# The last group's LoRA products computed densely over all experts, from tables kept in the place of W

## The chip, the cores and the metric

The kernel runs on one NeuronCore of a Trainium2 chip. TensorE (PE) multiplies matrices into PSUM, VectorE (DVE) and ScalarE (ACT) work on SBUF and PSUM, GpSimd (POOL) does small elementwise work and issues the indirect DMAs, SyncE (SP) issues most of the other DMAs. The metric is the device time of one execution in microseconds (us), as the median of several runs. Everything is in fp32, except the attention's parts, which are marked fp32r.

## The reference, cut to what matters

A graph-attention layer and a router-gated LoRA layer, each with a residual, for 128 batch elements of 128 rows by 1024 columns. The change concerns the second layer:

```python
def _gates(cls, router_w):                       # cls: row 0 of each batch element
    logits = jnp.einsum('bh,eh->be', cls, router_w)
    top_vals, top_idx = jax.lax.top_k(logits, 2)
    mask = jnp.full_like(logits, -jnp.inf)
    mask = mask.at[rows, top_idx].set(top_vals)
    return jax.nn.softmax(mask, axis=1)          # zero outside the two best of 8 experts

x = x + gnn(layernorm(x), adj, W, a)             # attention, 128 batch elements
z = layernorm(x)
gates = _gates(z[:, 0, :], router_w)             # (128, 8)
down = jnp.einsum('blh,erh->bler', z, lora_down) # 8 experts, rank 16
x = x + z + jnp.einsum('bler,ehr,be->blh', down, lora_up, gates)
```

(The last line is the reference's two residual steps written as one.) Only two of the eight gates of a batch element are nonzero, so two experts, 32 rows of the 128 of all experts, are enough for each of them.

## The kernel before, in words

A batch element i is one tile of 128 rows by 1024 columns (`xn`). Tiles go in pairs: pair q holds tiles 2q and 2q+1, and there are 64 pairs (`NQ`). Four tiles make a group g, and there are 32 groups (`NG`). The projection of a pair by W is a Strassen scheme with seven products (`product_1` to `product_7`, L312 to L343); each is eight fp32 matmuls (L293) of 128x128 weights with 260 moving columns. W lies in SBUF in seven blocks of one tile `w_sb` (B11, B21, B22, T1, T2, T3, NT4; L82, L83). Product 1 is the only one to read B11, product 2 the only one to read B21.

The order of the work is written out by hand. The loop over q at L633 fills eight lists, `gaps[0]` to `gaps[7]`, with small steps; L684 to L688 run the list of a gap and then the next product of pair q, so that the steps stand between the products. From q of 1 on, the order of the products is 1, 6, 2, 5, 7, 3, 4. While pair q is projected, pair q-1 goes through the attention: `attention_weights` (L376), `attend` (matmuls L406), `update` (L416, the exponential L423, L424, L425), `second_stats` (mean and variance, L229, and on POOL L233 to L443), and `turn`, which brings the tile's transpose to `y_t` by a DMA transpose (L458, issued on SP) and a copy on ACT (`rejoin`, L462). The last pair has no products after it and goes another way: `turn_at_end` (L465) transposes on PE (L472) and copies on ACT (L473). `join` (L478, ACT) adds the normalised tile to the residual.

A group's LoRA steps follow its second pair. `logits` and `choose` (L481 to L515) find the two best experts; `spread` (L520) lays them out by tile; `ratio` (L526, ACT) and `weigh` (L532 to L535, DVE) make the two gates. In the next pass of the loop `fetch` (L547) spreads the experts' numbers over the partitions (`to_rows`, L540 to L544), computes row numbers (L552, L555) and has POOL issue nine indirect DMAs: eight that gather each slot's down table from a DRAM table (`down`, L558), and one that gathers the up rows (`up`, L562). `gates` brings the gates to the partitions in the same way, `ffn_down` (L577) makes the lower products with four tiles of the group side by side in the PE array (32 columns each), scales them by the gates (L583, ACT), and `ffn_up` (L593) makes the upper products, again four side by side in 32 rows each. L597 on DVE adds them to the tile, and L600 on SP stores the finished tile, 512 KB.

For groups 0 to 30 all this lies between the products of later pairs. For group 31 there are none left: passes q = 64 and q = 65 of the loop run without a product.

PSUM is in two pools: `ps_w`, two buffers for the products, and `ps_m`, four buffers for all else.

Of the kernel before, what the change touches and what calls it, by code (L numbers as in the profile page):

```python
# [8 lines left out]
F32 = mybir.dt.float32  # L9
# [5 lines left out]
ALU = mybir.AluOpType  # L15
# [10 lines left out]
def adj_ffn_kernel(  # L26
# [13 lines left out]
    nc = tc.nc  # L40
    B, N, D = x.shape
    P = 128
# [449 lines left out]
    def choose(g):  # L492

        st = GRP[g]
        both = small.tile([G, E + 1], F32, tag="lg", name="lg")
        nc.vector.tensor_copy(both, st["pl"][:G, 0:E + 1])
        lg, dev = both[:, 0:E], both[:, E:E + 1]
        top = small.tile([G, 8], F32, tag="top", name="top")
        nc.vector.max(out=top, in_=lg)

        val = small.tile([G, 2, TOP], F32, tag="val", name="val")
        first = small.tile([G, E], F32, tag="first", name="first")
        mark = small.tile([G, 2, E], F32, tag="mark", name="mark")
        for s in range(TOP):
            nc.vector.scalar_tensor_tensor(mark[:, s], lg, top[:, s:s + 1], order,
                                           op0=ALU.is_equal, op1=ALU.mult)
            if s:
                nc.vector.tensor_scalar(first, order, val[:, 0, 0:1], None, op0=ALU.is_equal)
                nc.vector.scalar_tensor_tensor(mark[:, s], first, float(-E), mark[:, s],
                                               op0=ALU.mult, op1=ALU.add)  # L510
            nc.vector.tensor_reduce(val[:, 0, s:s + 1], mark[:, s], AX.X, ALU.max)
        st["experts"] = spread(val[:, 0], "experts")
        pr = small.tile([G, 2], F32, tag="pr", name="pr")
        nc.vector.tensor_sub(pr[:, 0:1], top[:, 1:2], top[:, 0:1])
        st.update(val=val, pr=pr, dev=dev)  # L515
# [12 lines left out]
    def weigh(g):  # L528

        st = GRP[g]  # L530
        gate, pr = st["val"][:, 1], st["pr"]
        nc.vector.tensor_scalar(gate[:, 0:1], pr[:, 1:2], 1.0, None, op0=ALU.add)  # L532
        nc.vector.reciprocal(gate[:, 0:1], gate[:, 0:1])
        nc.vector.tensor_mul(gate[:, 1:2], pr[:, 1:2], gate[:, 0:1])
        st["gates"] = spread(gate, "gates")  # L535

    def to_rows(own, name):

# [62 lines left out]

    def weights_3_main():
        nc.gpsimd.tensor_tensor(w_sb[:, T3, :, :, MAIN], w_sb[:, B22, :, :, MAIN],
                                w_sb[:, T1, :, :, MAIN], ALU.subtract)
# [26 lines left out]
    for q in range(NQ + 2):  # L633
        gaps = [[] for _ in range(8)]
        if q == 0:
            prepare(gaps)
        g, part = divmod(q - 2, 2)
        ffn = 0 <= g < NG
        if ffn and not part:
            gaps[6] += [(logits, g), (choose, g)]  # L640
        if q < NQ:
            gaps[6] += [(high, q, 3), (high, q, 1)]
            gaps[7].append((high, q, 2))
        if ffn and not part:
            gaps[6].append((ratio, g))
        if 0 < q <= NQ:
            i = 2 * q - 2
            gaps[0].append((attention_weights, q - 1))
            gaps[1] += [(attend, i), (update, i)]
            gaps[2] += [(attend, i + 1), (second_stats, i)]  # L650
            gaps[3].append((second_stats, i + 1))
            if q < NQ:
                gaps[2] += [(turn, i), (update, i + 1)]
                gaps[3].insert(0, (turn, i + 1))
                gaps[4].append((rejoin, i))
                gaps[5].append((rejoin, i + 1))
            else:
                gaps[2] += [(turn_at_end, i), (update, i + 1)]
                gaps[3].insert(0, (turn_at_end, i + 1))
            gaps[5] += [(join, i), (join, i + 1)]  # L660
        if q + 1 < NQ:
            gaps[3].append((first_stats, 2 * q + 2))
            gaps[4] += [(pair_sums, q + 1), (first_stats, 2 * q + 3)]
        if ffn and part:
            gaps[0].insert(0, (fetch, g))
            gaps[0].append((weigh, g))
            gaps[3].insert(0, (gates, g))
            gaps[4].insert(0, (ffn_down, g))
            gaps[5].insert(0, (ffn_up, (g, 0)))
            gaps[6].append((ffn_up, (g, 1)))  # L670
        if q % 2 == 0 and q < NQ:
            gaps[5].append((group_adj, q // 2))
            if q // 2 + 1 < NG:
                gaps[5].append((load_adj, q // 2 + 1))
        if q < NQ:
            gaps[3].insert(0, (low, q, 0))
            gaps[6] += [(low, q, 3), (low, q, 1)]

        if q + 1 < NQ:
            load_xt(q + 1)  # L680
            load_x(q + 1)
        if q == 1:
            slot, down_row, up_row = experts()
        products = project(q) if q < NQ else iter(())  # L684
        for gap in gaps:
            for f, *args in gap:
                f(*args)
            next(products, None)  # L688
# [37 lines left out]
```

## Time and profile before

| | before |
|---|---|
| median of three runs | 1979.18 us (1979.04 to 1979.5) |
| the profiled execution | 1979.41 us, of which the trace spans 1977.4 us |
| PE busy | 1933.0 us, 98% |
| DVE, ACT, POOL busy | 1666.3, 1075.3, 857.1 us |
| mean granted PE clock | 0.99 of full speed |
| last product of the last pair begins | 1925.79 us |
| last DVE instruction ends | 1971.81 us |

The table's first rows are times of whole executions; the rest is read from one profiled execution, whose microseconds count from its first instruction. A share of busy time is a mean over the whole span: 98% for PE says that the 64 passes with products are bound by PE, and nothing of the last 50 us. In the profile an fp32 matmul shows as two PE instructions, each with its own weight load (PEld), so eight fp32 matmuls stand as x16.

### The profile page before, as it was taken

Reading aid. Unit: us, or ns where it says so; the run is one execution under the profiler, and the core shown is the slowest. Engines: PE = TensorE matmul, PEld = TensorE weight load, DVE = VectorE, ACT = ScalarE, POOL = GpSimd, SP = SyncE. Lnnn points to the kernel's source line nnn. Section 1 sums busy time; section 2 is a strip of 40 time slices with the busy share of each in tenths; the row PEclk is TensorE's granted clock in tenths of the full one; section 3 lists DMA queues with packets and bytes.
Section 4 is the critical chain, followed back from the end, with each engine's and each line's share of the span. In section 5 each row is a group of like instructions: output and inputs, shape, how many; then the busy total and the mean of one; then the engine's idle time right before and its main releaser. Section 6 shows DMA issues by size and latency. Waiting matters only on the chain.

```text
span 1977.4 us, 30159 instructions
## 1 busy us (share of the span) xinstructions
PE 1933.0 (98%) x11028; PEld 1572.8 (80%) x11028; DVE 1666.3 (84%) x3515; ACT 1075.3 (54%) x1027; POOL 857.1 (43%) x1137
## 2 busy tenths in 40 slices
PE   7999999999999999999999999999999999999994
PEld 4888888888888888888888888888888888888882
DVE  8788888888888888888888888888888888888874
ACT  0365565565565565565565565565565565555561
POOL 4353443553443553443553443554443554433532
PEclk9999999999999999999999999999999999999995
DMA  5346556556556556556656556546556656556532
GB/s 192 117 129 192 175 149 187 166 143 192 176 150 187 165 145 192 176 150 187 172 138 194 176 148 186 175 135 195 175 151 186 176 133 199 171 152 185 180 77 102
DMA packets 345221, 324.99 MB, mean 164 GB/s; under 512 B 274289, under 2 KB 279409, under 8 KB 345073
## 3 DMA queue, kind: packets, MB, share of 16 engines
q1 hardware_dynamic: 325202, 278.45, 48.2%
q0 software_dynamic: 17408, 41.96, 7.2%
q10 hardware_dynamic: 2464, 2.65, 0.4%
q8 instruction: 88, 1.44, 0.3%
q14 instruction: 59, 0.48, 0.1%
HBM read 189.31 MB, written 67.63 MB: 130 GB/s over the span
## 4 chain that ended last, share of the span: by engine, by line
PE 90%; DVE 5%; DMA 2%; ACT 1%; issue 0%; POOL 0%; POOLq 0%; ACTq 0%; DVEq 0%
PE pw L293 75%; PE ph L406 6%; PE pu L593 4%; PE pd L577 3%; DMA tt<-halves 1%; PE pb L540 1%; PE pl L486 1%; DVE xn L424 1%; DVE xn L425 1%; DVE hp L416 1%; ACT y_t L462 1%; DMA w_sb<-in_w 1%; ACT halves L456 1%; DVE w_sb L169 0%; DVE stats L229 0%
## 5 line engine op out<-in xcount | busy, mean ns | idle before, releaser
L293 PE MATMUL pw<-w_sb,xt 128*128 128x260 f32 x4096 | 947.4, 386 | 2.4 <-DVE parts L364 1.7
L293 PEld LDWEIGHTS pw<-w_sb,xt 128*128 128x128 f32 x4096 | 767.5, 190 | 148.3 <-issue 29.6
L293 PE MATMUL pw<-w_sb,s 128*128 128x260 f32 x3072 | 711.2, 385 | 4.2 <-DVE w_sb L613 3.4
L293 PEld LDWEIGHTS pw<-w_sb,s 128*128 128x128 f32 x3072 | 578.1, 190 | 117.2 <-issue 17.4
L233 POOL TENSOR_SCALAR rstd<-mv 128x2 f32<-128x2 f32 x128 | 29.0, 227 | 869.4 <-DVE mv L230 864.2
L462 ACT COPY y_t<-tt 128x2048 uint16<-128x2048 uint16 x126 | 315.1, 2505 | 77.0 <-DMA tt<-halves 76.6
L558 POOL DMA_INDIRECT down<-table,at_down x256 | 259.5, 1014 | 168.6 <-DVE e L380 89.2
L229 DVE BATCH_NORM_STATS2 stats<-xn 128x6 f32<-128x512 f32 x512 | 324.1, 675 | 5.6 <-DMA xn<-in_x 5.5
L456 ACT COPY halves<-xn 128x2048 uint16<-128x2048 uint16 x126 | 239.8, 1903 | 119.6 <-DVE xn L425 73.7
L360 ACT ACTIVATE parts<-wh,rstd 128x512 fp32r<-128x512 f32 x192 | 133.9, 716 | 227.5 <-DVE wh L301 227.5
L423 ACT ACTIVATE ex<-hp 128x1024 f32<-128x1024 f32 x128 | 135.5, 1058 | 178.2 <-DVE hp L416 171.9
L597 DVE SCALAR_TENSOR_TENSOR xn<-pu,rstd,xn 128x512 f32<-128x512 f32 x256 | 174.5, 744 | 37.4 <-PE pu L593 37.3
L416 DVE TENSOR_TENSOR hp<-ph,att 128x512 f32<-128x512 f32 x256 | 161.4, 672 | 9.9 <-PE ph L406 9.6
L425 DVE SCALAR_TENSOR_TENSOR xn<-ex,xn 128x1024 f32<-128x1024 f32 x128 | 156.8, 1225 | 14.0 <-DVE xn L424 0.9
L406 PE MATMUL ph<-parts,adj_f 128*128 128x512 f32 x512 | 164.2, 442 | 1.3 <-ACT parts L360 0.8
L424 DVE SCALAR_TENSOR_TENSOR xn<-hp,xn 128x1024 f32<-128x1024 f32 x128 | 156.9, 1226 | 4.4
L478 ACT ACTIVATE xn<-xn,off,mul 128x1024 f32<-128x1024 f32 x128 | 151.3, 1230 | 0.8 <-POOL off L443 0.8
L364 DVE SCALAR_TENSOR_TENSOR parts<-wh,rstd,parts 128x512 fp32r<-128x512 f32 x192 | 138.9, 751 | 12.5 <-ACT parts L360 12.5
L301 DVE TENSOR_TENSOR wh<-pw,u 128x520 f32<-128x520 f32 x128 | 89.1, 696 | 48.8 <-PE pw L293 45.5
L301 DVE TENSOR_TENSOR wh<-pw,p 128x520 f32<-128x520 f32 x64 | 44.8, 700 | 80.9 <-PE pw L293 80.9
L406 PEld LDWEIGHTS ph<-parts,adj_f 128*128 128x128 f32 x512 | 96.5, 189 | 20.4 <-ACT parts L360 1.2
L234 POOL TENSOR_TENSOR rstd<-rstd,half_pow 128x2 f32<-128x2 f32 x128 | 91.5, 715 | 10.6
(105 smaller groups left out, 1489.8 us busy)
## 6 DMA issues: line engine op xcount, KB each, us to landing
xn<-in_x SPq DMA_DIRECT2D x128, 512.0 KB
xt<-in_x_t SPq DMA_DIRECT2D x128, 512.0 KB
out_y<-xn SPq DMA_DIRECT2D x128, 512.0 KB
adj_f<-in_adj_t POOLq DMA_DIRECT2D x32, 256.0 KB
adj_i<-in_adj SPq DMA_DIRECT2D x32, 256.0 KB
down<-table,at_down POOLq DMA_INDIRECT x256
w_sb<-in_w ACTq DMA_DIRECT2D x8, 256.0 KB
w_sb<-in_w SPq DMA_DIRECT2D x8, 256.0 KB
```

Source lines behind the costliest of these rows:

```text
L229: nc.vector.bn_stats(st[:, h, :], X[i][:, h * HALF:(h + 1) * HALF])
L293: nc.tensor.matmul(dst[:, j, 0:QE], lhs[:, k, :], w_sb[:, rhs, k, j], start=(first and k == 0), stop=(k == KH - 1), skip_group_check=not f ...
L364: nc.vector.scalar_tensor_tensor(in_two(PARTS[q][:, 1, b]), block, rstd, in_two(PARTS[q][:, 0, b].bitcast(F32)), op0=ALU.mult, op1=ALU.sub ...
L406: nc.tensor.matmul(PH[i][h], GRP[g]["adj_f"][:, t, :], PARTS[q][:, s, NH * (i % 2) + h], start=(s == 0), stop=(s == 1))
L416: nc.vector.tensor_tensor(hp[:, h * HALF:(h + 1) * HALF].rearrange("p (h f) -> p h f", f=F), ph.rearrange("p (h f) -> p h f", f=F), att[:, ...
L424: nc.vector.scalar_tensor_tensor(xt, hp, 0.0, xt, op0=ALU.max, op1=ALU.add)
L425: nc.vector.scalar_tensor_tensor(xt, ex, 1.0, xt, op0=ALU.min, op1=ALU.add)
L456: nc.scalar.copy(halves, X[i].bitcast(U16).rearrange("p (d s) -> p s d", s=2))
L462: nc.scalar.copy(y_of(i).bitcast(U16).rearrange("p k (n s) -> p s k n", s=2), TT.pop(i).rearrange("p (s k) n -> p s k n", s=2))
L478: nc.scalar.activation(X[i], X[i], AF.Identity, bias=GRP[g]["off"][:, t:t + 1], scale=GRP[g]["mul"][:, t:t + 1])
L558: nc.gpsimd.indirect_dma_start(out=st["down"][:, j * R:(j + 1) * R].rearrange("p r k -> p (r k)"), out_offset=None, in_=table, in_offset=b ...
L597: nc.vector.scalar_tensor_tensor(y[:, cols], pu[t], st["rstd"][:, t:t + 1], y[:, cols], op0=ALU.mult, op1=ALU.add)
```

## The change

It concerns group 31, the last one, alone. Groups 0 to 30 keep their steps.

- `load_all`: in pass q = 63, after product 1, SP issues two DMAs into block B11 of `w_sb`: the down table of all experts from DRAM (512 KB, in rows of 512 B) and the up table (512 KB, in rows of 4 KB). In SP's order they stand ahead of the DMA transposes of that pass.
- `order_all`: later in that pass ACT copies the down table into block B21 in the order that a matmul wants (128x1024).
- `down_dense`: the lower products with all 128 rows of the eight experts, unscaled, into one PSUM tile `pd_all`: tiles 0 and 1 of the group together (eight matmuls with 256 columns) after the last `attend` in pass 64, tile 2 (eight with 128 columns) ahead of the last tile's transposes, tile 3 (eight with 128 columns) after `logits`.
- `gates_dense`: gates for all eight experts, zero for six, made on four partitions (L635, L638 of the new file), turned to partitions by one small matmul (L641), copied (L644) and multiplied with `pd_all` (L646, DVE, 128x512).
- `up_dense`: for each tile and each half of the columns one matmul with 128 rows and 512 columns (L656), the addition on DVE (L657), and the store of that half, 256 KB, on SP or ACT.
- Without `fetch`, `gates`, `ffn_down` and `ffn_up`, group 31 has no indirect DMA, no L540 to L555 and no L577 to L600. `weigh` moves from pass 65 to the end of pass 64.

```diff
-        st["experts"] = spread(val[:, 0], "experts")
+        if g < NG - 1:
+            st["experts"] = spread(val[:, 0], "experts")
...
-        st["gates"] = spread(gate, "gates")
+        if g < NG - 1:
+            st["gates"] = spread(gate, "gates")
...
+    block = [w_sb[:, b].rearrange("p k j c -> p (k j c)") for b in (B11, B21)]
+    up_all = block[0][:, 0:D]
+    down_of_rows = block[0][:, D:2 * D].rearrange("p (e r k) -> p e r k", e=E, r=R)
+    down_all = block[1][:, 0:D].rearrange("p (k e r) -> p k e r", e=E, r=R)
+
+    def load_all():
+        nc.sync.dma_start(down_of_rows.rearrange("p e r k -> p e (r k)"),
+                          table.rearrange("(e p) c -> p e c", p=P))
+        nc.sync.dma_start(up_all, up_t)
+
+    def order_all():
+        nc.scalar.copy(down_all, down_of_rows.rearrange("p e r k -> p k e r"))
+
+    def down_dense(g, t, n):
+        st = GRP[g]
+        if t == 0:
+            st["pd"] = ps_w.tile([P, 2, HALF], F32, tag="pw", name="pd_all")[:, 0]
+        cols = slice(t * P, (t + n) * P)
+        for k in range(KC):
+            nc.tensor.matmul(st["pd"][:, cols], down_all[:, k].rearrange("p e r -> p (e r)"),
+                             st["y_t"][:, k, cols], start=(k == 0), stop=(k == KC - 1))
+
+    def gates_dense(g):
+        st = GRP[g]
+        val = st["val"]
+        chosen = small.tile([G, TOP, E], F32, tag="chosen", name="chosen", bufs=1)
+        for s in range(TOP):
+            nc.vector.tensor_scalar(chosen[:, s], order, val[:, 0, s:s + 1], val[:, 1, s:s + 1],
+                                    op0=ALU.is_equal, op1=ALU.mult)
+        rows = work.tile([G, E, R], F32, tag="hp", name="chosen_rows")
+        nc.vector.tensor_tensor(rows, chosen[:, 0, :, None].to_broadcast([G, E, R]),
+                                chosen[:, 1, :, None].to_broadcast([G, E, R]), ALU.add)
+        pg = ps_m.tile([P, HALF], F32, tag="pm", name="pg")
+        nc.tensor.matmul(pg[:, 0:G], rows.rearrange("g e r -> g (e r)"), ident[:G, :G],
+                         start=True, stop=True)
+        gate = small.tile([P, G], F32, tag="gate_all", name="gate_all", bufs=1)
+        nc.vector.tensor_copy(gate, pg[:, 0:G])
+        st["dn"] = work.tile([P, G, P], F32, tag="s1", name="dn_all", bufs=1)
+        nc.vector.tensor_tensor(st["dn"], st["pd"].rearrange("p (t n) -> p t n", t=G),
+                                gate[:, :, None].to_broadcast([P, G, P]), ALU.mult)
+
+    def up_dense(g):
+        st = GRP[g]
+        for t in range(G):
+            y = X.pop(g * G + t)
+            for h in range(NH):
+                cols = slice(h * HALF, (h + 1) * HALF)
+                pu = ps_m.tile([P, HALF], F32, tag="pm", name="pu")
+                nc.tensor.matmul(pu, st["dn"][:, t], up_all[:, cols], start=True, stop=True)
+                nc.vector.scalar_tensor_tensor(y[:, cols], pu, st["rstd"][:, t:t + 1], y[:, cols],
+                                               op0=ALU.mult, op1=ALU.add)
+                (nc.sync, nc.scalar)[h].dma_start(out[g * G + t, :, cols], y[:, cols])
...
         if ffn and not part:
             gaps[6].append((ratio, g))
+            if g == NG - 1:
+                gaps[6] += [(down_dense, g, 3, 1), (weigh, g)]
...
-        if ffn and part:
+        if q == NQ - 1:
+            gaps[1].append((load_all,))
+            gaps[5].append((order_all,))
+        if q == NQ:
+            gaps[2].insert(1, (down_dense, NG - 1, 0, 2))
+            gaps[3].insert(0, (down_dense, NG - 1, 2, 1))
+        if ffn and part and g == NG - 1:
+            gaps[0] += [(gates_dense, g), (up_dense, g)]
+        elif ffn and part:
             gaps[0].insert(0, (fetch, g))
             gaps[0].append((weigh, g))
             gaps[3].insert(0, (gates, g))
```

## The prediction

> **What bounds the kernel now.** The change touches only the last pass with products and what follows, so I read the end of the span. First the chain of waits in order of time (start us, us, what), from 1942 us on.
>
> ```profile
> 1942.58 1.98 PE pt L472 x8
> ...
> 1948.96 0.16 DVE val L533
> ...
> 1949.51 1.10 POOL down L558
> ...
> 1958.45 2.50 DMA down<-table,at_down
> ...
> 1961.08 3.41 PE pd L577 x58
> 1964.52 0.38 ACT dn L583
> 1964.94 1.22 PE pu L593 x8
> ...
> 1969.74 2.07 DVE xn L597 x3
> ```
>
> The gates' values are ready at 1949.30. Then POOL issues nine gathers one after the other, the last needed one lands at 1960.95, and only then do the bulk of the lower products run: from 1949.5 to 1964.5 nothing else is on the path. Second, the timeline of PE and ACT in that end (start us, us, idle before in brackets).
>
> ```profile
> 1932.33 0.97 PE L406 MATMUL ph<-parts,adj_f 128*128 128x512 f32 x3 [0.49 <-DVE parts L364]
> ...
> 1937.36 1.94 PE L472 MATMUL pt<-ident,xn 128*128 128x128 f32 x8 [4.07 <-DVE xn L425]
> ...
> 1942.58 1.97 PE L472 MATMUL pt<-ident,xn 128*128 128x128 f32 x8 [3.28 <-DVE xn L425]
> ...
> 1945.96 2.37 ACT L478 ACTIVATE xn<-xn,off,mul 128x1024 f32<-128x1024 f32 x2 [0.79 <-POOL off L443]
> ...
> 1948.24 0.28 ACT L526 ACTIVATE pr<-pr,lg 4x1 f32<-4x1 f32 x1
> ```
>
> PE is idle for 4.07 us before the first tile's transposes and 3.28 us before the second's; the new products are put there. The gates' ratio (L526) stands behind ACT's two joins, not behind the logits. Third, short windows (us, busy us of PE, PEld, DVE, ACT, POOL; then clock, DMA share, GB/s).
>
> ```profile
> 1933.00:1933.50 0.50, 0.29 (x2) 0.00 (x0) 0.38 (x3) 0.00 (x0) 0.00 (x0) 0.93 0.00 0
> 1933.50:1934.00 0.50, 0.00 (x0) 0.00 (x0) 0.50 (x2) 0.00 (x0) 0.00 (x0) 0.50 0.00 0
> ...
> 1964.00:1964.50 0.50, 0.48 (x10) 0.17 (x2) 0.00 (x0) 0.00 (x0) 0.00 (x0) 0.85 0.00 0
> ...
> 1967.50:1968.00 0.50, 0.50 (x3) 0.37 (x2) 0.50 (x2) 0.00 (x0) 0.00 (x0) 0.56 0.00 0
> ```
>
> The clock falls to half at about 1933.43, rises at 1964.15 and falls at 1967.56. The last two are 3.41 us apart, and the first lies nine times 3.41 us before the second. The finished tiles leave at 401 to 410 GB/s from 1970.43 to 1975.6.
>
> **What the Trainium skill says.** "TensorE: Matmul & The Clock Gate", Part 1: the clock is full or half, decided on free-running windows of about 3.4 us; the steps above fit it. "FP8 and Floating Point Precision", TensorE Precision Notes: true fp32 takes four passes through the array. Four times 260 columns at the 2.4 GHz of the first page is 433 ns; the trace's products start every 3.5 us for eight, 437 ns each. It agrees. "TensorE: Matmul & The Clock Gate", Part 3: tiles side by side run together, so dense products give that up. The trace agrees: 32 lower products with 32 columns take 1.98 us at 1914.32. "DMA: Bandwidth & Descriptors", Bandwidth: 1 MB into SBUF takes 6.15 us when issued from GpSimd; no row of before shows such a load from SP at this place.
>
> **The change part by part**, on the trace's clock. A 260-column half matmul (one x of x16) takes 0.219 us, so 0.84 ns a column at full and 1.68 at half clock.
>
> *Loads.* Product 1 of pair 63 ends at 1901.2. SP waits for it and then issues two loads of 512 KB. Behind them on SP stand the two DMA transposes, which waited for ACT until 1908.09 in before. At the skill's 6.15 us and 1 us of issue the loads land at about 1908.5 (estimate); from below, at 406 GB/s, at 1905. One gather or transpose may be pushed by 1 us. Who would notice: pair 63's lower products at 1914.32, whose last gather was issued at 1909.46 and lands 2.5 us later (as in the tail), with 2.3 us to spare; ACT's copies of the transposes, which began at 1916.64, behind L583. I take zero, bounds 0 and +3.
>
> *order_all.* One ACT copy, 128x1024; the rows of such size are 1.06 (L423) and 1.23 us (L478). It runs between 1923.7 and 1925.6, where ACT was idle 1.25 us; behind it are two L360, whose reader on DVE (L364) starts only at 1928.52. Zero.
>
> *Lower products.* Tiles 0 and 1: 16 halves of 256 columns, 16 x 0.215 = 3.4 us at full clock from 1933.3, done at 1936.8, before 1937.36: free. With the fall at 1933.43 as in this trace: eight halves at 0.43 until the next window's end (1936.87), eight at 0.215 after it, done at 1938.6. Then the first transposes are 1.2 us late and ACT's two copies with them; ACT's exponential L423 (1940.04) stands behind these copies and ends at about 1942.2, and DVE's L425 is 0.9 us late. Tile 2: 128 columns do not hide the weight load. The nearest row is L204 of the start, the same form: 16 halves from 62.9 to 66.4, 0.233 each, so 16 x 0.233 = 3.7 us, half of it after each ACT copy (1939.07, 1939.93): done at 1942.9, 0.3 us after the second tile's transposes could start. Together the last tile's chain is 0 to 1.4 us late; the logits had 0.9 us to spare before L526 (choice done 1947.35, L526 at 1948.24). I take +0.9 for L526 in this phase, 0 in the best. Tile 3: 3.7 us from 1945.6, done at 1949.4, before the small gate matmul.
>
> *Removed.* Between L526's end (1948.52) and the first upper product (1964.94) lie 16.4 us: L540 to L555, L520, nine gathers, pd, dn. *Added in their place:* weigh, three small DVE steps (0.55 us with gaps, rows L532 to L534); two chosen and the rows (0.16, 0.2, 0.3); the matmul's round trip DVE to DVE (0.75, as L520's end to L542 at 1950.23); copy 0.16; dn_all 128x512 from PSUM 0.67 (L416's mean). With hand-overs of 0.1 the sum is 3.1 us: upper products start at 1951.65.
>
> *Upper products.* Before: 1964.94 to the last DVE end at 1971.81, 6.87 us, paced by DVE. After: 16 halves of 512 columns one after the other, 16 x 0.43 = 6.9 us, plus a drain of 0.2 and one DVE step of 0.75: 7.85 us; DVE needs 8 x 0.69 = 5.5 and is not the bound. At full clock the last DVE ends at 1959.5. In the trace's phase 0.9 later, and one window at half costs four halves' worth, 1.7 us: 1962.1.
>
> *Stores.* Before, four stores of 512 KB came at once: bytes begin 0.87 us after the first DVE end (1969.56), run 5.2 us, and the span ends 1.8 us after the last byte, 5.6 after the last DVE. Now 256 KB leave every 0.86 us, 305 GB/s, under 406: no queue, so 0.87 + 0.65 + 1.8 = 3.3 us after the last DVE. A gain of 2.3.
>
> *Sum.* End of span 1962.8 (full clock) to 1965.4 (this phase), against 1977.4: -14.6 to -12.0. The runs are about 1.8 us above the span (median 1979.18), so 1964.6 to 1967.2. I take 1966.5, as the trace's own phase is the likelier.
>
> **Rivals.** *A cold PE.* If half clock holds throughout: tiles 0 and 1 take 6.8 us (to 1940.2), the exponential ends at 1943.9, L526 at 1951.35 (2.8 late), upper products run from 1954.5 for 13.8 us, the last DVE ends at 1969.2 and the span at 1972.5: 1974.3 us. For: before ran the whole of 1933.5 to 1964 at half. Against: the new products fill PE from 1933.3 to 1949.4, and 3 us of full work raised the clock at 1964.15. *A collision of loads with the gathers of pair 63*, which holds PE at 1914.32: up to 3 us, 1969.5. Against: the gathers keep POOL's pace of 1.25 us each and the DMA share is 0.11 to 0.34 there. *Slower: the table load lands late.* ACT's second L478 of pass 63 now waits for it, and behind it stand L617, two L360 and so the last attention. It decides from 1924.7 on (1928.5 less 1.2 + 1.2 + 1.4), microsecond for microsecond. The gain of 12.7 is used up and 4 us lost at a landing of 1941.4, 40 us for 1.05 MB, 26 GB/s. For: rows of 512 B and transposes behind it. Against: the gathers have the same rows and run at 66 GB/s while held by POOL's issue; at that rate it lands at 1917.5. That group 31 keeps its fetch is excluded: the built program has nine POOL DMAs fewer.
>
> **How the numbers follow.** The forecast has 0.76 (own range 1964 to 1969), the cold PE 0.12 (1969 to 1975), the collision 0.05 (1967 to 1970), the late load 0.04 (over 1983), and 0.03 for causes that leave it within 0.2%. That bound, 4 us, is about what a measurement of this kernel can tell from no change. The range, 1963 to 1971, leaves out the late load, the worst of the cold PE and the no-change case. Faster: 0.76 + 0.05 + 0.11; same: 0.03 + 0.01; slower 0.04.
>
> **What would show it.** No POOL work after 1946; pd_all's first x16 right behind ph, ended by 1937 to 1939; the first pu at 1951 to 1953; pu as x16 in about 7 to 9 us, with DVE waiting for PE; the span's end 3.3 us after the last DVE. Wrong: a PE idle before 1926 that before doesn't have, L617 starting after 1925, or the clock at 0.5 through pu.

## The result, and the profile after

The changed kernel takes 1968.17 us (median of six runs, 1967.21 to 1969.25); the kernel before, beside it, 1979.34 us (six runs, 1979.04 to 1980.88). The ratio is 0.9941, with a 95% interval of 0.9928 to 0.9954, so the change saves 11.2 us. (A later comparison of the same two kernels, shown under "The combination, and once more", has 14.0 us.) The forecast of 1966.5 us is 1.7 us too low, and the result lies in the range of 1963 to 1971.

The profiled execution of the new kernel spans 1965.7 us (its own run took 1968.2). The chain of waits at its end (start us, us, what), against the chain of before that the prediction shows:

```profile
1948.94 1.23 ACT xn L478
1950.16 0.19 ACT pr L527
...
1951.66 0.39 PE pg L641 x2
1952.05 1.01 issue
1953.06 8.82 PE pu L656 x16
1961.88 0.02 issue
1961.90 0.75 DVE xn L657
```

No DMA is left in it. From ACT's second join (L478) the chain goes through the ratio (L527), the small DVE steps and the gate matmul (L641) to sixteen upper products in one run, and PE's upper products, not DVE's additions, now set the last stretch. The entry called "issue" is the copy of the gates and the multiplication that makes `dn_all`, which this view does not name.

The timeline of PE and ACT in the same end (start us, us, engine, line, operation; idle before in brackets):

```profile
1925.44 2.04 ACT L617 COPY w_sb<-w_sb 128x1024 f32<-128x1024 f32 x1
...
1934.98 3.62 PE L626 MATMUL pd_all<-y_t,w_sb 128*128 128x256 f32 x16
1939.20 1.06 PE L472 MATMUL pt<-ident,xn 128*128 128x128 f32 x8 [0.61 <-DVE xn L425]
1940.50 2.05 PE L626 MATMUL pd_all<-y_t,w_sb 128*128 128x128 f32 x16 [0.24 <-ACT y_t L473]
1944.51 1.06 PE L472 MATMUL pt<-ident,xn 128*128 128x128 f32 x8 [1.96 <-DVE xn L425]
...
1947.20 3.50 PE L626 MATMUL pd_all<-y_t,w_sb 128*128 128x128 f32 x16
1947.79 2.37 ACT L478 ACTIVATE xn<-xn,off,mul 128x1024 f32<-128x1024 f32 x2 [1.54 <-POOL off L443]
1950.07 0.28 ACT L527 ACTIVATE pr<-pr,lg 4x1 f32<-4x1 f32 x1
...
1953.06 8.80 PE L656 MATMUL pu<-w_sb,dn_all 128*128 128x512 f32 x16 [1.03 <-issue]
```

The three L626 rows are the lower products of tiles 0 and 1, of tile 2 and of tile 3. The idle of 4.07 us ahead of the first tile's transposes has become 0.61, and the last lower product ends at 1950.70, about 1 us before the gate matmul. Tile 3's products are of the same shape as tile 2's and took 3.50 us instead of 2.05: they ran at half clock for all but about the last 0.45 us. The windows show when, and they are laid so that they fall on the steps of the clock (us, busy us of PE, PEld, DVE, ACT, POOL; then clock, DMA share, GB/s):

```profile
1940.00:1943.42 3.42, 2.32 (x19) 1.89 (x17) 3.25 (x6) 2.00 (x3) 0.00 (x0) 1.00 0.00 0
1943.42:1946.83 3.41, 1.76 (x24) 1.34 (x24) 2.44 (x4) 1.07 (x2) 0.73 (x2) 1.00 0.00 0
1946.83:1950.25 3.42, 3.18 (x16) 3.15 (x17) 1.32 (x9) 2.46 (x3) 0.75 (x4) 0.50 0.00 0
1950.25:1953.66 3.41, 1.42 (x8) 0.93 (x8) 1.97 (x8) 0.10 (x1) 0.00 (x0) 1.00 0.00 0
1953.66:1957.07 3.41, 3.41 (x6) 1.33 (x5) 1.50 (x2) 0.00 (x0) 0.00 (x0) 0.50 0.20 77
```

After a window in which PE was busy for 1.76 of 3.41 us the clock is at half for the next one, after 3.18 of 3.42 it is at full, after 1.42 at half again. The upper products begin at 1953.06 and run at half through the last window shown.

**Where the time came from.** To compare executions I count from the start of the last product (L293) of pair 63, which is the last thing that all kernels do alike: 1925.79 in before, 1927.63 in after. From there (us):

| stretch | before | after | difference |
|---|---|---|---|
| to the start of the ratio (L526, L527) | 22.45 | 22.44 | 0 |
| start of the ratio to the first upper product | 16.70 | 2.99 | -13.71 |
| first upper product to the end of the last addition on DVE | 6.87 | 9.60 | +2.73 |
| last addition to the end of the span | 5.59 | 3.04 | -2.55 |
| sum | 51.61 | 38.07 | -13.54 |

The span is shorter by 11.7 us only (1977.4 to 1965.7), since this execution of after reached the last product 1.84 us later. Most of that loss is at the other end of the run. One product of pair 0, which waits for DVE's sums of W's blocks, in before and then in after (timeline, columns as above):

```profile
40.52 3.77 PE L293 MATMUL pw<-w_sb,s 128*128 128x260 f32 x16 [3.37 <-DVE w_sb L613]
```

```profile
40.77 5.46 PE L293 MATMUL pw<-w_sb,s 128*128 128x260 f32 x16 [3.61 <-DVE w_sb L672]
```

Two windows of after there, columns as before:

```profile
38.79:42.20 3.41, 1.43 (x7) 1.25 (x8) 3.38 (x4) 0.00 (x0) 0.00 (x0) 1.00 0.00 0
42.20:45.61 3.41, 3.41 (x9) 2.66 (x8) 2.13 (x2) 0.00 (x0) 0.00 (x0) 0.50 0.00 0
```

PE waits for these sums in both kernels. In after's execution most of that idle time fell into one clock window (1.43 of 3.41 us busy), so the next one was at half, which costs 1.7 us. A second window at half, from 66.10 to 69.52, costs another 0.4 us. Both are a matter of the phase of the windows and not of the change: of the thirteen executions traced for this document, eight have a long product at 40 us (5.20 to 5.46 us), among them two built on the kernel before, and five have 3.77 us, among them kernels that differ from after only from pair 63 on. The second window came in two of the thirteen, of which one is built on before. Such a scatter would also explain why the kernel before has a median of 1979.34 us here and of 1980.89 to 1981.14 in the comparisons below; the one trace of it has the short product, so this is not shown.

### The profile page after: what moved, and what is told of

It is laid out like the page before. It is cut to its first block, busy times and chain, and to the rows that moved or that the text cites. A ratio compares the mean times of both kernels' runs of the same rounds, so it can differ in the third digit from the quotient of the medians.

```text
span 1965.7 us, 30104 instructions
## 1 busy us (share of the span) xinstructions
PE 1939.8 (99%) x11010; PEld 1578.3 (80%) x11010; DVE 1663.5 (85%) x3512; ACT 1077.6 (55%) x1027; POOL 847.4 (43%) x1128
## 3 DMA queue, kind: packets, MB, share of 16 engines
q8 instruction: 87, 1.43, 0.3%
## 4 chain that ended last, share of the span: by engine, by line
PE 95%; DVE 3%; DMA 1%; ACT 1%; issue 0%; POOL 0%; POOLq 0%; DVEq 0%
PE pw L293 80%; PE ph L406 6%; PE pu L595 3%; PE pd L579 3%; PE pb L542 1%; PE pl L486 1%; DVE w_sb L169 1%; DMA tt<-halves 0%; PE pu L656 0%; DMA xn<-in_x 0%; DVE stats L229 0%; DVE prod L178 0%; DVE w_sb L192 0%; ACT y_t L462 0%; DVE xn L425 0%; DVE xn L424 0%
## 5 line engine op out<-in xcount | busy, mean ns | idle before, releaser
L293 PE MATMUL pw<-w_sb,xt 128*128 128x260 f32 x4096 | 947.9, 386 | 2.4 <-DVE parts L364 1.7
L293 PEld LDWEIGHTS pw<-w_sb,xt 128*128 128x128 f32 x4096 | 767.9, 190 | 148.4 <-issue 25.6
L293 PE MATMUL pw<-w_sb,s 128*128 128x260 f32 x3072 | 712.9, 385 | 4.4 <-DVE w_sb L672 3.6
L293 PEld LDWEIGHTS pw<-w_sb,s 128*128 128x128 f32 x3072 | 579.2, 190 | 118.0 <-issue 21.2
L560 POOL DMA_INDIRECT down<-table,at_down x248 | 251.3, 1013 | 163.4 <-DVE e L380 89.7
L360 ACT ACTIVATE parts<-wh,rstd 128x512 fp32r<-128x512 f32 x192 | 134.3, 716 | 238.0 <-DVE wh L301 238.0
L599 DVE SCALAR_TENSOR_TENSOR xn<-pu,rstd,xn 128x512 f32<-128x512 f32 x248 | 169.0, 744 | 21.9 <-PE pu L595 21.9
L406 PE MATMUL ph<-parts,adj_f 128*128 128x512 f32 x512 | 164.3, 442 | 1.3 <-ACT parts L360 0.9
L478 ACT ACTIVATE xn<-xn,off,mul 128x1024 f32<-128x1024 f32 x128 | 151.4, 1233 | 1.5 <-POOL off L443 1.5
L364 DVE SCALAR_TENSOR_TENSOR parts<-wh,rstd,parts 128x512 fp32r<-128x512 f32 x192 | 138.8, 750 | 11.8 <-ACT parts L360 11.8
L406 PEld LDWEIGHTS ph<-parts,adj_f 128*128 128x128 f32 x512 | 96.5, 189 | 20.3 <-ACT parts L360 1.2
L234 POOL TENSOR_TENSOR rstd<-rstd,half_pow 128x2 f32<-128x2 f32 x128 | 91.3, 713 | 10.7
```

What stands on the lines that cost most here:

```text
L293: nc.tensor.matmul(dst[:, j, 0:QE], lhs[:, k, :], w_sb[:, rhs, k, j], start=(first and k == 0), stop=(k == KH - 1), skip_group_check=not f ...
L364: nc.vector.scalar_tensor_tensor(in_two(PARTS[q][:, 1, b]), block, rstd, in_two(PARTS[q][:, 0, b].bitcast(F32)), op0=ALU.mult, op1=ALU.sub ...
L406: nc.tensor.matmul(PH[i][h], GRP[g]["adj_f"][:, t, :], PARTS[q][:, s, NH * (i % 2) + h], start=(s == 0), stop=(s == 1))
L478: nc.scalar.activation(X[i], X[i], AF.Identity, bias=GRP[g]["off"][:, t:t + 1], scale=GRP[g]["mul"][:, t:t + 1])
L560: nc.gpsimd.indirect_dma_start(out=st["down"][:, j * R:(j + 1) * R].rearrange("p r k -> p (r k)"), out_offset=None, in_=table, in_offset=b ...
L599: nc.vector.scalar_tensor_tensor(y[:, cols], pu[t], st["rstd"][:, t:t + 1], y[:, cols], op0=ALU.mult, op1=ALU.add)
```

## The experiments

All kernels of one paragraph's comparison ran on the same chip beside the kernel before. Tails are counted as in the table above, in its four stretches, each from one traced execution; medians are of whole executions. The kernel after itself ran only in the first and in the last comparison; where another kernel is set against it, tails are compared. Four traces have after's end unchanged (after, its repetition, the kernel without loads and the one with contiguous reads); their tails are 38.05 to 38.26 us, so a difference of 0.2 us in a tail is no more than the phase of the clock makes.

**Which removed part paid: the gathers.** The kernel before, except that group 31 issues no gathers and uses the rows of group 30, which lie in SBUF.

```diff
+        if g == NG - 1:
+            st["down"], st["up"] = GRP[g - 1]["down"], GRP[g - 1]["up"]
+            return
         st["down"] = work.tile([P, G * TOP * R, KC], F32, tag="down", name="down", bufs=1)
```

> The kernel before, in which group 31 issues no gathers and reads the rows that were gathered for group 30 (so the gather of the last group's rows is left out). Theory, that the gathers were worth most of the gain and the lower products' place the rest: L577 starts at once after the gates' small matmul, its 64 halves take about 3.7 us at half clock, the upper products start about 6.2 us after the ratio (L526) ends instead of 16.4, the span falls by about 10, the time is 1969 us. Rival, that most of the gain came from the new place of the lower products and the gathers would have been hidden otherwise: at most 5 us, 1974 or more.

Measured: 1970.3 us (1969.0 to 1970.7, before on that chip 1980.89, 1978.79 to 1982.3; ratio 0.9945, 0.9928 to 0.9961). Tail 22.44 + 6.03 + 6.86 + 5.60 = 40.93 us. The timeline of this run:

```profile
1952.10 3.66 PE L580 MATMUL pd<-y_t,down 128*32 128x128 f32 x64
1955.82 0.37 ACT L586 ACTIVATE dn<-pd,gate 128x128 f32<-128x128 f32 x1 [5.33 <-PE pd L580]
1956.24 1.14 PE L596 MATMUL pu<-up,dn 32*128 32x512 f32 x8 [0.48 <-ACT dn L586]
```

The expectation held: it is 1.3 us off in the time, and the upper products start 5.75 us after the ratio's end, where 6.2 was expected. The nine gathers alone were worth 10.68 us of the tail's 13.54: ratio to first upper product falls from 16.70 to 6.03. What is left there is the spreading of the gates (until 1952.10), the packed lower products, 3.66 us, and their scaling. The dense form takes another 3.04 us off that stretch, by having the lower products done before the gates are known, and gives back 2.74 us in the next one. So the dense arithmetic as such bought nearly nothing here beyond making the gathers unnecessary; the rest of the gain over this kernel is the stores.

**The stores by halves.** The kernel before, except that group 31's outputs leave as halves of 256 KB, the first halves from SP and the second from ACT.

```diff
-            if h:
+            if g == NG - 1:
+                (nc.sync, nc.scalar)[h].dma_start(out[g * G + t, :, cols], y[:, cols])
+            elif h:
                 nc.sync.dma_start(out[g * G + t], X.pop(g * G + t))
```

> The kernel before with one part of the change alone: group 31's finished tiles are stored by halves of 256 KB, on SP and ACT in turn, as soon as each half is done. Theory, that the stores by halves are a gain of their own of 2 to 2.5 us: the span ends 3.0 to 3.3 us after the last DVE instruction instead of 5.6, 1977 us. Rival, that 5.6 us is a fixed cost of the program's end: no change, 1979.2.

Measured: 1978.76 us (1976.38 to 1980.38 over 20 runs, before 1980.89 over 23; ratio 0.9989, 0.9982 to 0.9995). Tail 22.44 + 16.86 + 7.02 + 3.11 = 49.43. The last additions and the stores in its timeline:

```profile
1968.65 5.64 DVE L597 SCALAR_TENSOR_TENSOR xn<-pu,rstd,xn 128x512 f32<-128x512 f32 x8 [15.87 <-PE pu L593]
1969.47 2.30 SPq L600 DMA_DIRECT2D out_y<-xn  x4
...
1972.06 2.64 ACTq L600 DMA_DIRECT2D out_y<-xn  x4
```

SP's first store is issued at 1969.47, 0.8 us into the additions; in before no store of this group could start until both halves of a tile were there. The end after the last addition is 3.11 us in place of 5.59, and the whole tail 2.18 us shorter, which the medians show too (2.1). The last stretch is about as short with either form of the products (3.11 here, 3.04 in after), so I add the gain to that of the gathers: 10.68 + 2.18 = 12.86 of 13.54. No kernel had these two edits and no other.

**Whether the loads cost anything.** After, without the two loads in pass 63.

```diff
         if q == NQ - 1:
-            gaps[1].append((load_all,))
             gaps[5].append((order_all,))
```

> The changed kernel without the two loads of the tables (order_all and the products read what product 1 left there, so group 31's LoRA part is left out in effect). Theory, that 1 MB of loads in pass 63 is hidden: within 0.5 us of the changed kernel from the last product on, about 1968. Rival, that the loads hold back the gathers or transposes of pair 63 and cost 1 to 3 us: 1965 to 1967, and the stretch from pair 63's first product to its last shorter by as much.

Measured: 1967.96 us (1966.29 to 1968.69; ratio 0.9936, 0.9919 to 0.9953). Tail 22.45 + 3.24 + 9.42 + 3.15 = 38.26, after's being 38.07. Pair 63's products take 28.06 us from the start of the first to that of the last in before, 28.05 in after and 28.06 here. The loads are free; the collision that the prediction named as a rival did not come.

**What hiding the lower products is worth.** After, with all four tiles' lower products together behind the logits instead of in the last attention.

```diff
-                gaps[6] += [(down_dense, g, 3, 1), (weigh, g)]
+                gaps[6] += [(down_dense, g, 0, 4), (weigh, g)]
...
-        if q == NQ:
-            gaps[2].insert(1, (down_dense, NG - 1, 0, 2))
-            gaps[3].insert(0, (down_dense, NG - 1, 2, 1))
```

> The changed kernel with all lower products after the logits, as eight matmuls of 512 columns, instead of amid the last attention. Theory, that their place among PE's idle gaps is worth what they would take on the path: 16 halves of 0.43 us at full and 0.86 at half clock, done 8 to 10 us after the logits, so upper products 3.4 to 5.2 us later, partly given back by a warm clock in them (about 1.7): 1970 to 1972. Rival, that their place is worth nothing, since the gates come late anyway: 1968.

Measured: 1971.05 us (1970.17 to 1972.7; ratio 0.9952, 0.9935 to 0.9968), 3.1 above the run without loads on the same chip. Tail 22.44 + 8.71 + 7.90 + 3.05 = 42.10, 4.03 more than after. Its timeline:

```profile
1947.06 10.05 PE L626 MATMUL pd_all<-y_t,w_sb 128*128 128x512 f32 x16
...
1958.45 7.11 PE L656 MATMUL pu<-w_sb,dn_all 128*128 128x512 f32 x16 [1.03 <-issue]
```

The lower products, which ran at half clock until 1952.96, delay the upper products by 5.7 us, somewhat more than the 3.4 to 5.2 expected. But behind 10 us of unbroken PE work the upper products run at full clock, 7.11 us in place of 8.80, and 1.7 us come back. The gain of the placing is the difference. This run is also the clean measure of the upper products: 7.90 us to the last addition, where the prediction's term for full clock was 7.85.

**Whether the half clock can be avoided.** After's upper products lose 1.7 us to one window at half, and tile 3's lower products lose 1.45. Here filler matmuls (256 columns, into a spare tile that nothing reads) were put behind tile 2's products (three), behind tile 3's (two) and behind the gate matmul (two):

```diff
+    def warm(n):
+        if "pf" not in GRP:
+            GRP["pf"] = ps_w.tile([P, 2, HALF], F32, tag="pw", name="pf")
+        for _ in range(n):
+            nc.tensor.matmul(GRP["pf"][:, 0, 0:256], ident, up_all[:, 0:256], start=True,
+                             stop=True)
...
+        warm(2)
         gate = small.tile([P, G], F32, tag="gate_all", name="gate_all", bufs=1)
...
-                gaps[6] += [(down_dense, g, 3, 1), (weigh, g)]
+                gaps[6] += [(down_dense, g, 3, 1), (warm, 2), (weigh, g)]
...
+            gaps[3].insert(1, (warm, 3))
```

> The changed kernel with seven filler matmuls of 256 columns into a spare PSUM buffer: three after tile 2's lower products, two after tile 3's, two after the gates' small matmul. They compute nothing that is used. Theory, that the upper products lost one window of 3.41 us to half clock because PE stood nearly idle for 2.4 us ahead of them: L656 takes 7.1 us instead of 8.8, the time is 1.7 us under the changed kernel's, about 1966.5. Rival, that the upper products' length is set by DVE or by the stores: 8.8 us still, no gain, or a loss where the fillers hold back L641.

Measured: 1967.49 us (1965.98 to 1967.74, before on that chip 1981.13; ratio 0.9933, 0.9916 to 0.9949). Tail 22.44 + 3.56 + 8.82 + 3.02 = 37.85, 0.2 below after, which is nothing by the measure given above. Its timeline:

```profile
1945.92 2.05 PE L626 MATMUL pd_all<-y_t,w_sb 128*128 128x128 f32 x16
...
1947.81 1.03 PE L634 MATMUL pf<-w_sb,ident 128*128 128x256 f32 x4
...
1950.70 1.87 PE L634 MATMUL pf<-w_sb,ident 128*128 128x256 f32 x4
1952.36 8.03 PE L665 MATMUL pu<-w_sb,dn_all 128*128 128x512 f32 x16
```

The first fillers did their work: tile 3's products take 2.05 us. But then PE has nothing to do from 1948.8 to 1950.4, while ACT computes the ratio and DVE the gates, and the clock falls at 1950.94; the last fillers then run at half (1.87 us for four halves) and themselves stand ahead of the upper products. Neither the 1.7 us nor the unchanged 8.8 us that were expected came: the fillers left one hole of 1.55 us, and that was enough for the clock to fall.

**The ratio ahead of the last join.** ACT computes the ratio behind its two joins (L478). Here the last tile's join is put behind the ratio.

```diff
             if g == NG - 1:
+                gaps[6].append((join, G * NG - 1))
                 gaps[6] += [(down_dense, g, 3, 1), (weigh, g)]
...
-            gaps[5] += [(join, i), (join, i + 1)]
+            gaps[5] += [(join, i)]
+            if q < NQ:
+                gaps[5] += [(join, i + 1)]
```

> The changed kernel with the last tile's join (L478) moved behind the gates' ratio (L527) on ACT. Theory, that the ratio waits for ACT's two joins and not for the logits: it starts about 1.2 us earlier, then PE's third part of the lower products (to 1950.7 on the changed kernel's clock) becomes what L641 waits for, so upper products start 0.9 us earlier and the time falls by about 0.9. Rival, that the chain through logits and choice sets the ratio: no change.

Measured: 1966.24 us (1964.93 to 1967.72; ratio 0.9928, 0.9911 to 0.9945). Tail 21.31 + 3.58 + 9.87 + 3.00 = 37.76. Its timeline:

```profile
1945.21 3.78 PE L626 MATMUL pd_all<-y_t,w_sb 128*128 128x128 f32 x16
...
1946.95 0.28 ACT L527 ACTIVATE pr<-pr,lg 4x1 f32<-4x1 f32 x1
...
1948.92 0.59 PE L641 MATMUL pg<-ident,chosen_rows 4*128 4x4 f32 x2
1950.53 9.09 PE L656 MATMUL pu<-w_sb,dn_all 128*128 128x512 f32 x16 [1.03 <-issue]
```

The ratio is 1.13 us earlier (21.31 for 22.44), but the gate matmul now waits for tile 3's lower products, which run at half clock until 1948.99, so that the upper products start only 0.54 us earlier; they are again at half for a part. The tail gains 0.31, where 0.9 was expected. Another wait took the place of the one removed.

**Both together.**

> Both edits, fillers and the join behind the ratio. Theory: the gains add, 2.5 us under the changed kernel, about 1965.6, the best of all versions. Rival, that the earlier ratio only uncovers the lower products of tile 3 and the fillers behind them: no better than the fillers alone.

Measured: 1964.45 us (1962.6 to 1965.01; ratio 0.9915, 0.9898 to 0.9931). Tail 21.31 + 3.03 + 7.90 + 3.08 = 35.32, 2.75 below after. Its timeline:

```profile
1946.85 2.05 PE L626 MATMUL pd_all<-y_t,w_sb 128*128 128x128 f32 x16
1948.73 1.03 PE L634 MATMUL pf<-w_sb,ident 128*128 128x256 f32 x4
1950.17 0.38 PE L649 MATMUL pg<-ident,chosen_rows 4*128 4x4 f32 x2 [0.41 <-DVE chosen_rows L646]
1950.48 1.13 PE L634 MATMUL pf<-w_sb,ident 128*128 128x256 f32 x4
1951.62 7.11 PE L665 MATMUL pu<-w_sb,dn_all 128*128 128x512 f32 x16
```

Each edit alone gave 0.2 and 0.3 us; together they give 2.75. The forecast was about this size, but as a sum of two gains that neither kernel showed alone. Each edit removes what made the other useless: with the fillers tile 3 is done before the gates want PE, and with the earlier ratio the hole before the gate matmul is 0.41 us, so the clock stays at full to the end.

**Reads that step.** `order_all` took 2.04 us where the prediction's rows of that size had 1.06 and 1.23, and the 128-column products took 0.128 us a half where the prediction had 0.233, from L204. Both L617 and L204 read their source in steps of 32 bytes. Here both read the elements in the order in which they lie.

```diff
-            nc.tensor.matmul(pc, mean_of, down_sb[:, :, :, k], start=(k == 0), stop=(k == KC - 1))
+            nc.tensor.matmul(pc, mean_of, down_sb[:, k], start=(k == 0), stop=(k == KC - 1))
...
-        nc.scalar.copy(down_all, down_of_rows.rearrange("p e r k -> p k e r"))
+        nc.scalar.copy(block[1][:, 0:D], block[0][:, D:2 * D])
```

> The changed kernel with two reads made contiguous that step by 32 bytes: order_all's copy (L617, then in the wrong order) and the moving side of the table's means at the start (L204, then the wrong sums), so the LoRA tables are wrong in effect. Theory, that the step of 32 bytes and not the 128 columns made both slow: L617 falls from 2.04 to about 1.1 us, L204's halves from 0.233 to about 0.12 us, which takes 1.8 us off PE at the start and nothing off at L617: 1966.4. Rival, that L204's halves are bound by the load of 128 weight columns: 0.233 still, and the time unchanged.

Measured: 1965.76 us (1963.54 to 1966.75; ratio 0.9925, 0.9909 to 0.9942). First L204 in after, then L204 and L617 here:

```profile
64.82 3.95 PE L204 MATMUL pc<-down_sb,mean_of 128*128 128x128 f32 x16
```

```profile
62.81 2.03 PE L204 MATMUL pc<-down_sb,mean_of 128*128 128x128 f32 x16
...
1921.35 1.04 ACT L617 COPY w_sb<-w_sb 128x1024 f32<-128x1024 f32 x1
```

The copy falls from 2.04 to 1.04 us and the sixteen halves from 3.95 to 2.03, both to half. The strided halves do not follow the clock: they take 3.96 us in before at full clock, and 3.95 in after, where the clock is at half from 66.10 on. The tail is 38.05, after's 38.07: L617's second microsecond was hidden, as the prediction had it for the first. L204's two microseconds stay: the last product of pair 63 starts at 1923.55, and at 1925.64 and 1926.35 in the two other traces of this comparison that have the short product at 40 us.

**The combination, and once more.** After and the kernel with both edits were run again, on one chip, beside a third in which L204's means come from two matmuls of 512 contiguous columns and a reduction of each on DVE. The diff is against the kernel with both edits.

```diff
-        pc = ps_m.tile([P, E, R], F32, tag="pm", name="pc")
-        for k in range(KC):
-            nc.tensor.matmul(pc, mean_of, down_sb[:, :, :, k], start=(k == 0), stop=(k == KC - 1))
+        flat = down_sb.rearrange("p e r k -> p (e r k)")
+        pc = work.tile([P, E, R], F32, tag="hp", name="pc")
+        for h in range(NH):
+            ph = ps_m.tile([P, HALF], F32, tag="pm", name="pc_h")
+            nc.tensor.matmul(ph, mean_of, flat[:, h * HALF:(h + 1) * HALF], start=True, stop=True)
+            nc.vector.tensor_reduce(pc[:, h * E // NH:(h + 1) * E // NH],
+                                    ph.rearrange("p (e r k) -> p e r k", e=E // NH, r=R), AX.X,
+                                    ALU.add)
```

> The changed kernel once more, beside the two best versions on one chip. Theory, that its runs differ from one another by the phase of PE's clock windows, at the start (product 6 of pair 0 with 3.77 or 5.46 us) and in the upper products (7.1 to 9.1 us): the tail from the last product's start to the end is 38.1 us within 0.5, the ratio to before 0.9941 within 0.0007. Rival, that the first comparison flattered or understated it: a tail outside 37.5 to 39.

> Fillers and the join behind the ratio once more. Theory: 2.7 us under the changed kernel, a tail of 35.3 us. Rival, that the first profile caught a lucky phase: a tail of 37 or more, 1 us or less under it.

> As before, and the table's means at the start made from two matmuls with 512 contiguous columns and two reductions on DVE in place of eight matmuls that step by 32 bytes. It computes all of the reference. Theory: L204 falls from 3.95 to about 1.9 us on PE, and since PE is what bounds the passes with products, all of it is gained: 2.0 us under the version with fillers and the moved join. Rival, that DVE's two reductions (about 1.3 us) hold back the steps of pair 1 behind them: no gain, or a loss of up to 1 us.

| kernel (before on that chip: 1981.14, nine runs) | median us (five runs) | ratio, 95% | tail us |
|---|---|---|---|
| after | 1967.12 (1966.59 to 1967.67) | 0.9931 (0.9917 to 0.9944) | 38.05 |
| fillers and earlier ratio | 1964.16 (1963.48 to 1964.87) | 0.9916 (0.9902 to 0.9929) | 35.25 |
| the same, and contiguous means | 1963.03 (1962.02 to 1965.02) | 0.9911 (0.9898 to 0.9925) | 35.32 |

After saves 14.0 us here. Its tail repeats to 0.02 us, but the ratio of 0.9931 misses the 0.9941 within 0.0007 that was expected: from one comparison to the next, the time of the whole is less certain than that. The fillers with the earlier ratio repeat their tail to 0.07 us, and their runs do not overlap after's: 3.0 us less in the medians, 2.8 in the tail. The contiguous means do shorten their own step:

```profile
64.49 1.96 PE L206 MATMUL pc_h<-down_sb,mean_of 128*128 128x512 f32 x4
```

That is 1.96 us for 3.95, but the last product of pair 63 starts only 0.9 us earlier than in the run without it (1925.98 for 1926.85), and the runs of the two kernels overlap. The trace shows where the other microsecond went. The two reductions (0.69 us each) now stand ahead of DVE's next steps, so the attention step L385 starts at 69.14, only 1.0 us earlier than the same step in the run without them (L380, 70.16). PE is 1.7 us ahead of that run right behind L206, and 1.0 us at the next logits (L491, at 116.75). That is the rival of the expectation, and the kernel with contiguous reads, which has no reductions, keeps its 2 us.

## Why the prediction was right, step by step

The mechanism held: the chain through POOL's gathers is gone, dense products hide in PE's idle stretches, and nothing took the gathers' place for as long. That the time came so near is in part luck, since errors cancel. Its terms, one by one, counted from the start of the last product where the prediction gave a time (its own clock less 1925.79):

- *Loads, zero (0 to +3).* Right, shown by the kernel without them. The bytes had landed by about 1908.5 in after, some 5 us after the first issue at 1903.38; the prediction's estimate allowed 7.3 us from the end of product 1, so from SP the two loads were faster than it had priced them. The first transposes were issued 17.70 us before the last product in both kernels, so SP was not held up.
- *order_all, zero, of 1.06 to 1.23 us.* Zero is right, the size is wrong: 2.04 us. Counted from the last product, it delays one L360 by 1.9 us, and the reader of that (L364) did not wait. The Trainium skill, "SBUF — State Buffer", Door 1: The DMA port swizzle, notes that SBUF's lines are 16 bytes long and that fp32 can be strided for free only up to four elements. A step of 32 bytes is beyond that, and the 1.04 us of the contiguous copy agrees with it. I had taken the size into account, and not the access pattern.
- *Tiles 0 and 1, 3.4 us at full clock.* 3.62 us, and free: the first transposes start 11.57 us after the last product in both kernels. The sum for before's phase had the clock fall ahead of them. It fell there in all four traces without these products at this place and in none of the nine with them, whatever the phase. In the kernel with fillers that window begins 4.11 us after the last product's start, 4.22 in before, and the clock stayed up. The step overlooked that the new products begin early enough to fill a part of the window that decides.
- *Tile 2, 3.7 us.* Here a step failed: 2.05. The row that priced it, L204, is slow not for its 128 columns but for its 32-byte step. At 0.128 us a half these products are close to L199's at the start, whose sixteen halves of 8 columns take 1.85 us, 0.116 each; that row was the nearest one. The error made no difference to the end: PE was idle for 1.96 us between these products and the second transposes.
- *L526 late by 0.9 in this phase, 0 in the best.* Zero (22.44 for 22.45). The 0.9 followed from the clock's fall and from tile 2's size, and neither came as priced.
- *Tile 3, 3.7 us.* 3.50, at half clock, where the prediction's 3.7 was tile 2's price at full clock: right by two errors that cancel. At full clock it is 2.05. It was done before the gate matmul, as forecast.
- *From the ratio's end to the upper products, 3.1 us.* 2.71.
- *Upper products, 7.85 us and 1.7 for one window at half, 9.55.* 9.60 in after, and 7.90 at full clock in the three kernels that reach it. That one window at half would come was taken from before's phase, and after had another. In the four traces with after's end the products themselves (L656) took 8.56 to 8.80 us, so about one window was lost in each; but it was lost because PE idles ahead of them, which the prediction did not say, so the right size was partly luck.
- *Stores, 3.3 us after the last addition instead of 5.6.* 3.04, a gain of 2.55 for the 2.3 forecast; by themselves they are worth 2.18 of the tail.
- *Sum.* On the common count the forecast's end of span was 37.0 (full clock) to 39.6 (this phase); measured 38.07.

The whole was 1.7 us too low because of two things outside this sum. The prediction let the start of the last product stand where before had it, and after's execution reached it 1.84 us later, mostly by the two windows at half clock at 42 and 66 us, which no step considered (1.69 and 0.43 us; the product at 40 us also began 0.25 us later, and about 0.5 us was regained on the way). And it took the runs 1.8 us above the span, where the traced run of after is 2.5 above its span (1968.2 to 1965.7). Against that, the tail is 0.85 us shorter than the 38.9 that 1966.5 stood for: 1.84 + 0.7 - 0.85 = 1.7.

Of the rivals, the cold PE came in part: half clock for two windows of those that count, not throughout. (In its sum, 1951.35 is the end of L526, not its start; the rest follows from it rightly.) The collision and the late load did not come, which the kernel without loads shows. One of the signs of being wrong, L617 starting after 1925, is there by the letter (1925.44), but counted from the last product it lies at 1923.60 of before's clock: the whole run is late by then, not the load.

## What to carry to other kernels

When a chain of small transfers stands between a late decision and the end, computing everything that could be chosen and scaling what wasn't chosen by zero can pay even at four times the arithmetic, as long as the arithmetic goes where the engine is idle; what paid here was the transfers that became unnecessary (10.7 of 13.5 us), and with the lower products behind the logits 4 us of it would have been lost again. Price an operation from a row with the same access pattern and not only of the same shape: a step of 32 bytes doubled both a copy and a matmul. Near the end of a kernel, look at each 3.41-us window of PE's clock: two edits that gain nothing alone can be worth 2.8 us together when one fills the window and the other closes the hole.

## What the runs showed of the hardware

- **The clock falls well before PE is idle, and the share of busy time doesn't tell when.** The Trainium skill, "TensorE: Matmul & The Clock Gate", Part 1, has the clock fall after an idle window of about 3.4 us. The length of the window agrees; that it has to be idle does not. Windows of 3.41 us with PE busy for 0.42 (1.42 and 1.43 us), 0.52 (1.76) and 0.57 (1.94 us, 1930.02 to 1933.43 in before) of their length were each followed by one at half. But after's windows from 35.39 (1.77 us busy) and from 45.63 (1.69) were followed by one at full, and this one, busy throughout, by one at half:

```profile
62.69:66.10 3.41, 3.41 (x25) 3.25 (x24) 2.03 (x4) 0.72 (x1) 3.03 (x6) 1.00 0.45 117
66.10:69.52 3.42, 3.42 (x15) 3.23 (x14) 0.71 (x1) 0.00 (x0) 0.43 (x3) 0.50 1.00 394
```

  Its PE work is mostly L199, whose halves have 8 columns and take 0.116 us, and L204 with its 32-byte step. What the array is given to do fits better. As an estimate I take 0.84 ns of work for a column of an fp32 half at full clock (from the 0.219 us for 260 columns), half of that for L406 (fp32r, 512 columns every 0.23 us), twice as much at half clock, each times the share of the 128x128 array that the matmul uses. By this count the window above holds 0.34 of its length in work. Over all windows of the thirteen traces, some 7,400, the clock fell after those with up to 0.38 (27 times) and stayed up after those with 0.40 and more; at half clock it rose after 0.76 and more (22 times) and stayed after 0.66 and less. The count was made afterwards, on the traces that it describes; no run was made to test it.
- **The phase of these windows against the program varies by execution**, and with it the product at 40 us: 3.77 us or 5.20 to 5.46. The runs of one kernel scatter by 1 to 4 us, and a single pair of traces can show such a difference as if it were an effect.
- **Reads in steps of 32 bytes take twice as long**, on ACT (2.04 for 1.04 us, 128x1024) and for PE's moving operand (0.247 for 0.127 us a half of 128 columns). On PE the strided time is the same at full and at half clock (3.96 and 3.95 us for sixteen halves).
